# Transforming back along the rows by even and odd frequencies, with the halves as sum and difference and the poles' part included

## The chip, the cores and the metric

The kernel runs on one core of a Trainium2 chip. TensorE (PE) multiplies matrices into PSUM; VectorE (DVE), ScalarE (ACT) and GpSimd (POOL) work on SBUF, and all but POOL also on PSUM in this kernel. SyncE (SP) issues DMAs, and POOL issues some too. The metric is the device time of one execution in microseconds (us), the median of several; lower is better.

## The reference

The input is `x`, 16 images of 16 channels of 256 x 256, float32. Two layers run one after the other, each on a group-normed input and with a residual sum. The change is in layer 0, a Laplace-type layer:

```
alpha = jnp.fft.fft2(x, axes=(-2, -1))
...
output_residue1 = jnp.einsum('biox,oxik->bkox', alpha, S)
output_residue2 = jnp.einsum('bikpq,ikpq->bkpq', D, weights_residue)
x1 = jnp.fft.ifft2(output_residue1, s=(Ny, Nx), axes=(-2, -1)).real
...
F = jnp.einsum('kbpq,bipz->kbiqz', output_residue2, E1)
x2 = jnp.einsum('kbiqz,biqx->kizx', F, E2).real
return x1 + x2 / Nx / Ny
```

`x1` is an inverse transform over both axes; `x2` is the poles' part, a sum of exponentials `E1` along the rows' axis (y) times `E2` along x. Layer 1 (convolutions and a gate) follows and isn't changed; it needs `x + x1 + x2/N/N`, group-normed.

## The kernel before, in words

The program has four stages, one function each, and the change touches the first three.

`layer0_forward` norms the input, transforms it along y and then along x, and writes the spectrum `al` to DRAM. Beside that, a generator `tables` makes tables piece by piece; the last of them are the exponentials of the poles (lines 500 to 531): for each axis and each pair of channels `k` some twenty DVE operations, an exponential and a sine, and at L529 the product `arg`, 128 x 2 x 256, which goes to the DRAM table `ed`. On the axis "2" the factor `last`, +-1/(N*N), is multiplied in.

`layer0_mix` goes through 33 groups of four y frequencies, mixes channels, and transforms back along x in `columns` (L682 to L715): for each frequency `fy` and each half `q` of the batch, PE gives an even and an odd part, ACT copies the odd one (L701), DVE writes sum and difference into `o` (L704, L705; tag `h`, five buffers), and POOL issues the DMA to the DRAM array `hd` (L709; L715 for fy = 0 and 128). Here `hd` is `[128 fy, batch, channel, v, 256 x]`, where v is the real or imaginary part. In this stage the order on PE, ACT, DVE and POOL is that of the program text.

`layer0_back` (L779 to L868) transforms back along y. For each of 16 images it loads the residues `r2`, and then goes through four groups of four channels, 64 groups in all. For a group SP loads `h` (1 MB, from `hd`, one DMA) and `x` (1 MB). For each pair of channels one product with `e1` gives `pf`, which ACT copies to `f` (L834). For each channel PE makes `py`, 128 x 2 x 256: each half image `yh` takes three matmuls, two with the table `iy` over v (L839) and one with `f` and `e2` for the poles' part (L842). DVE adds `py` into `x` (L845) and takes its statistics (L846). After four channels the statistics are aggregated (L849), and `group_norm_scalars` (L30 to L54) makes mean and scale for the two norm groups: two matmuls with `ones` (L34, L42), small DVE operations of 128 x 2 (L36 to L39, L44, L47, L50 to L53) and a square root on ACT (L46). Then DVE and POOL each write two of the four channels, normed, into `z` (L856), and SP stores `z` to the DRAM array `zn` (L865). `h` and `x` have three buffers each, `py` three, `f` three, `z` three. In this stage no order is written out by hand: the framework orders the instructions of each engine when the program is built, and SP's DMAs stand in one queue.

`layer1` reads `zn`.

Of the kernel before, what the change touches and what calls it, by code (L numbers as in the profile page):

```python
# [10 lines left out]
F32 = mybir.dt.float32  # L11
I32 = mybir.dt.int32
AF = mybir.ActivationFunctionType
ALU = mybir.AluOpType
# [4 lines left out]
C = 16  # L19
N = 256  # L20
G = 8
P = 128
# [34 lines left out]
def load(nc, pool, src, shape, name):  # L57
    t = pool.tile(shape, F32, tag=name, name=name)
    nc.sync.dma_start(out=t, in_=src)
    return t  # L60
# [322 lines left out]
def tables(ctx, tc, d, psum, tabs):  # L383

    nc = tc.nc
    td, avd, ed = tabs
    cp = ctx.enter_context(tc.tile_pool(name="tc", bufs=1))
# [23 lines left out]
    for k in range(C):  # L411
        e = tp.tile([P, N], F32, tag="te", name="te")
# [89 lines left out]
    for i, axis in enumerate("12"):  # L502
        pr = cp.tile([P, C], F32, name=f"epr{axis}")
        pi = cp.tile([P, C], F32, name=f"epi{axis}")
        for a in range(2):
            nc.sync.dma_start(out=pr[64 * a : 64 * a + 64], in_=d[f"p{axis}r_kp"])
            nc.sync.dma_start(out=pi[64 * a : 64 * a + 64], in_=d[f"p{axis}i_kp"])
        tr = cp.tile([P, N], F32, name=f"etr{axis}")
        nc.sync.dma_start(out=tr, in_=d["ty" if axis == "1" else "tx"].to_broadcast([P, N]))
        for k in range(0, C, 2):  # L510
            arg = tp.tile([P, 2, N], F32, tag="arg", name="arg")
            n = tp.tile([P, 2, N], F32, tag="n", name="n")
            nf, af = n.rearrange("p k x -> p (k x)"), arg.rearrange("p k x -> p (k x)")
            for j in range(2):
                nc.vector.tensor_scalar(arg[:, j], tr, pi[:, k + j : k + j + 1], None, ALU.mult)

            nc.vector.tensor_scalar(n, arg, 1.0 / TWO_PI, phase, ALU.mult, ALU.add)
            nc.vector.tensor_scalar(n, n, ROUND, ROUND, ALU.add, ALU.subtract)
            nc.vector.scalar_tensor_tensor(af, nf, -c1, af, ALU.mult, ALU.add)
            nc.vector.scalar_tensor_tensor(af, nf, -c2, af, ALU.mult, ALU.add)  # L520
            nc.vector.tensor_scalar(arg, arg, turn, None, ALU.add)
            nc.vector.tensor_scalar(arg, arg, 3.1415925, -3.1415925, ALU.min, ALU.max)
            nc.scalar.activation(n, arg, AF.Sin)
            for j in range(2):
                nc.vector.tensor_scalar(arg[:, j], tr, pr[:, k + j : k + j + 1], None, ALU.mult)
            exponential(nc, tp, af)
            if axis == "2":
                nc.vector.tensor_scalar(n, n, last, None, ALU.mult)
            nc.vector.tensor_tensor(arg, arg, n, ALU.mult)  # L529
            nc.sync.dma_start(out=ed[:, i, k : k + 2], in_=arg)  # L530
            yield

# [15 lines left out]
def layer0_mix(ctx, tc, d, al, hd, tabs):  # L548
# [133 lines left out]
    def columns(g, f, yt):  # L682

        ph = [psh.tile([P, 2, N], F32, tag="ph", name="ph") for q in range(2)]
        for e in range(2):
            if e:
                yield
            for n, (c, v) in enumerate(((0, 0), (0, 1), (1, 0), (1, 1))):
                i = 2 * (2 * c + e) + v
                for q in range(2):  # L690
                    lanes = slice(64 * q, 64 * q + 64)
                    nc.tensor.matmul(  # L692
                        ph[q][:, e],
                        lhsT=yt[lanes, i].rearrange("p t k -> p (t k)"),
                        rhs=ix[lanes, i],
                        start=n == 0,
                        stop=n == 3,
                    )
        for q in range(2):
            odd = hp.tile([P, 2, P], F32, tag="odd", name="odd", bufs=2)  # L700
            nc.scalar.copy(odd, ph[q][:, 1].rearrange("p (v x) -> p v x", v=2))  # L701
            o = hp.tile([P, 2, 2, P], F32, tag="h", name="h", bufs=5)
            even = ph[q][:, 0].rearrange("p (v x) -> p v x", v=2)
            nc.vector.tensor_tensor(o[:, :, 0], even, odd, ALU.add)  # L704
            nc.vector.tensor_tensor(o[:, :, 1], even, odd, ALU.subtract)  # L705
            o = o.rearrange("p v h x -> p v (h x)")
            fy = 4 * g + f
            if fy % P:
                nc.gpsimd.dma_start(  # L709
                    out=hd[fy, q:nb:2].rearrange("b k v x -> b (k v x)"),  # L710
                    in_=o.rearrange("p v x -> p (v x)"),
                )
            else:
                part = fy // P
                nc.gpsimd.dma_start(out=hd[0, q:nb:2, :, part], in_=o[:, 0])  # L715

    E = mybir.EngineType
    with tc.manual_schedule(engines={E.PE, E.Activation, E.DVE, E.Pool}):
# [60 lines left out]
def layer0_back(ctx, tc, d, hd, bd, zn, mr, ed):  # L779


    nc = tc.nc
    nb = d["x"].shape[0]
    cp = ctx.enter_context(tc.tile_pool(name="bc", bufs=1))
    iy = load(nc, cp, d["iy"], [P, 2, N], "iy")
    ones = load(nc, cp, d["ones"], [P, P], "ones")

    e1 = cp.tile([P, C, N], F32, name="e1")
    e2 = cp.tile([P, C, N], F32, name="e2")
# [22 lines left out]
    for b in range(nb):  # L812
        r2 = fp.tile([P, P], F32, tag="r2", name="r2")
        nc.sync.dma_start(out=r2, in_=bd[b])
        for k0 in range(0, C, 4):
            h = hp.tile([P, 4, 2, N], F32, tag="h", name="h")
            nc.sync.dma_start(
                out=h.rearrange("p k v x -> p k (v x)"),
                in_=hd[:, b, k0 : k0 + 4].rearrange("f k v x -> f k (v x)"),
            )  # L820
            x = hp.tile([P, 4, 2, N], F32, tag="x", name="x")
            nc.sync.dma_start(
                out=x.rearrange("p k h x -> p (k h) x"),
                in_=d["x"][b, k0 : k0 + 4].rearrange("k (h p) x -> p (k h) x", p=P),
            )
            st = sm.tile([P, 4, 6], F32, tag="st", name="st")
            for k in range(4):
                if k % 2 == 0:
                    pf = psf.tile([P, 2, N], F32, tag="pf", name="pf")
                    nc.tensor.matmul(  # L830
                        pf, lhsT=r2, rhs=e1[:, k0 + k : k0 + k + 2], start=True, stop=True
                    )
                    f = fp.tile([P, 2, N], F32, tag="f", name="f")
                    nc.scalar.copy(f, pf)  # L834
                py = psy.tile([P, 2, N], F32, tag="py", name="py")
                for yh in range(2):
                    ys = slice(P * yh, P * yh + P)
                    for v in range(2):
                        nc.tensor.matmul(  # L839
                            py[:, yh], lhsT=iy[:, v, ys], rhs=h[:, k, v], start=v == 0, stop=False  # L840
                        )
                    nc.tensor.matmul(  # L842
                        py[:, yh], lhsT=f[:, k % 2, ys], rhs=e2[:, k0 + k], start=False, stop=True
                    )
                nc.vector.tensor_tensor(x[:, k], py, x[:, k], ALU.add)  # L845
                nc.vector.bn_stats(st[:, k], x[:, k].rearrange("p h x -> p (h x)"))  # L846
            mv = sm.tile([P, 2, 2], F32, tag="mv", name="mv")
            for g in range(2):
                nc.vector.bn_aggr(mv[:, g], st[:, 2 * g : 2 * g + 2].rearrange("p c s -> p (c s)"))  # L849
            g0 = k0 // 2  # L850
            nm, rs = mr[:, b, g0 : g0 + 2, 0], mr[:, b, g0 : g0 + 2, 1]
            for _ in group_norm_scalars(nc, sm, psn, ones, mv, 2, nm, rs):
                pass
            z = zbuf[(4 * b + g0 // 2) % 3]
            for g, eng in ((0, nc.vector), (1, nc.gpsimd)):
                eng.tensor_scalar(  # L856
                    z[:, 2 * g : 2 * g + 2, :, 1 : N + 1],
                    x[:, 2 * g : 2 * g + 2],
                    nm[:, g : g + 1],
                    rs[:, g : g + 1],  # L860
                    ALU.add,
                    ALU.mult,
                )
            for h in range(2):
                nc.sync.dma_start(  # L865
                    out=zn[b, k0 : k0 + 4, 1 + P * h : 1 + P * h + P].rearrange("k p x -> p k x"),
                    in_=z[:, :, h],
                )  # L868
# [433 lines left out]
def fourier_tables():  # L1302
# [33 lines left out]
    for t in tt:  # L1336
# [5 lines left out]
        "wxa": parities(wx[..., :P]),  # L1342
        "wxn": wxn,
        "ix": ix,
        "iy": iy,
        "ones": np.full((P, P), 1.0 / P),
        "pair": np.stack([np.tile(np.eye(64), (2, 1)), -np.tile(np.eye(64), (2, 1))], axis=1),
        "gc": np.tile(np.repeat(np.eye(G), 2, axis=0), (8, 1)),
# [8 lines left out]
        "m8": np.tile(np.repeat(np.eye(8), M, axis=0), (4, 1)),  # L1357
        "mt": mt.reshape(P, 2, 16),
        "phase": np.repeat([0.25, 0.0], 64)[:, None],
        "last": np.repeat([1.0, -1.0], 64)[:, None] / (N * N),  # L1360
    }
    return {name: a.astype(np.float32) for name, a in out.items()}

# [25 lines left out]
def forward(ctx, tc, d):  # L1389
# [2 lines left out]
    keep = ctx.enter_context(tc.tile_pool(name="keep", bufs=1))  # L1392
    al = dram.tile([NF, 2, 64, nb, N], F32, name="al")
    bd = dram.tile([nb, P, P], F32, name="bd")
    hd = dram.tile([P, nb, C, 2, N], F32, name="hd")
    tabs = (
        dram.tile([P, 2, C, N], F32, name="td"),
        dram.tile([NF, P, 384], F32, name="avd"),
# [34 lines left out]
```

## Time and profile before

| | us |
|---|---|
| median of 8 runs | 7631.73 |
| range of the runs | 7622.29 to 7638.18 |
| the profiled execution's time | 7629.84 |
| its span | 7628.0 |

| engine | busy us | share of the span |
|---|---|---|
| PE | 7108.3 | 93% |
| DVE | 4905.9 | 64% |
| ACT | 3670.5 | 48% |
| POOL | 2833.3 | 37% |

The profile lists, for each engine, when it was busy and what ended its idle time. It cuts the span into 40 equal slices; a digit is a busy share in tenths. Instructions of one line, engine and shape form a group, with a count, busy time, mean duration in ns, and the idle time just before them. A table by windows gives the busy time of each engine between two points of the span, the clock that PE was granted, the share of the 16 DMA engines that was busy, and what they moved.

### The profile page before, as it was taken

What the parts mean: (1) busy time and instruction counts of PE and PEld (TensorE: products, weight loads), DVE (VectorE), ACT (ScalarE), POOL (GpSimd) and SP (SyncE); (2) the same over time, 40 slices, a digit from 0 to 9 for tenths busy, and PEclk for the clock granted to TensorE, in tenths of its full rate; (3) what the DMA queues carried; (4) which work ended last, traced back from release to release, by engine and by line L of the source; (5) the groups of instructions that cost most, each with busy time, mean ns of one, the idle gap of its engine ahead of it and who ended that gap; (6) DMA issues with size and microseconds to landing.
All of it is one profiled execution on the core that took longest, in us unless ns stands there. A gap on an engine that the chain in (4) does not pass through costs nothing. (4 is left out here: it accounts for less than half of the span.)

```text
span 7628.0 us, 147451 instructions
## 1 busy us (share of the span) xinstructions
PE 7108.3 (93%) x58728; PEld 4078.4 (53%) x58728; DVE 4905.9 (64%) x9184; ACT 3670.5 (48%) x5387; POOL 2833.3 (37%) x3616
## 2 busy tenths in 40 slices
PE   7889999799999998999979999999999999999997
PEld 5778888567666666777723333333333333333332
DVE  8999865366666665666656666666666666666652
ACT  2223333366666663111156565666565666565661
POOL 2334444211111111111145555555554555554552
PEclk9999999899999999999989999999999999999998
DMA  3344444333333335877757888898888898888886
GB/s 98 111 115 122 115 120 111 108 101 96 96 95 101 100 95 163 265 242 246 230 154 220 238 241 246 246 266 256 252 245 247 245 265 256 252 246 249 244 266 199
DMA packets 936290, 1442.20 MB, mean 189 GB/s; under 512 B 91866, under 2 KB 807958, under 8 KB 903606
## 3 DMA queue, kind: packets, MB, share of 16 engines
q1 hardware_dynamic: 792374, 958.51, 45.0%
q0 software_dynamic: 143232, 474.25, 19.6%
q8 instruction: 469, 7.68, 0.4%
q14 instruction: 215, 1.76, 0.1%
HBM read 875.87 MB, written 556.47 MB: 188 GB/s over the span
## 5 line engine op out<-in xcount | busy, mean ns | idle before, releaser
L1021 ACT ACTIVATE wide<-c,b 32x512 f32<-32x512 f32 x2176 | 1477.5, 679 | 372.3 <-PE c L972 319.9
L1049 DVE TENSOR_TENSOR t<-pd,r 64x512 f32<-64x512 f32 x1088 | 744.4, 684 | 1318.7 <-PE pd L1041 1294.2
L1052 DVE TENSOR_TENSOR top<-pd,t 32x512 f32<-32x512 f32 x2176 | 1504.3, 691 | 55.6 <-DMA cf<-top 2.8
L1115 PE MATMUL c2ps<-rows,c 128*32 128x512 f32 x12288 | 1394.5, 600 | 23.4 <-ACT e L1124 13.7
L972 PE MATMUL c<-z,w 102*128 102x512 f32 x2048 | 1051.7, 645 | 138.9 <-ACT wide L1021 115.2
L1033 POOL COPY wide<-wide 32x1031 f32<-32x1031 f32 (+1 forms) x576 | 569.0, 988 | 1385.2 <-ACT wide L1021 1357.9
L1041 PE MATMUL pd<-wide,dw 128*128 128x512 f32 x2048 | 1011.9, 616 | 7.7 <-POOL wide L1034 2.7
L1115 PEld LDWEIGHTS c2ps<-rows,c 128*32 128x32 f32 x12288 | 388.6, 109 | 996.8 <-issue 892.2
L972 PEld LDWEIGHTS c<-z,w 102*128 102x128 f32 x2048 | 398.6, 197 | 701.7 <-issue 513.5
L1041 PEld LDWEIGHTS pd<-wide,dw 128*128 128x128 f32 x2048 | 376.2, 194 | 628.7 <-issue 454.2
L709 POOL DMA_DIRECT2D hd<-h x254 | 188.6, 742 | 1271.5 <-DVE h L705 1251.7
L1124 ACT ACTIVATE e<-c2ps,b 128x512 f32<-128x512 f32 x256 | 175.9, 687 | 862.2 <-PE c2ps L1115 859.5
L1034 POOL COPY wide<-wide 32x1031 f32<-32x1031 f32 (+1 forms) x576 | 572.4, 994 | 35.8
L313 PE MATMUL px<-wxn,u 128*64 128x256 f32 x4224 | 558.8, 385 | 3.0 <-ACT o L320 2.5
L839 PE MATMUL py<-h,iy 128*128 128x256 f32 x2048 | 542.2, 383 | 5.2 <-issue 5.2
L635 PE MATMUL ps<-tt,lt 128*64 128x256 f32 x4224 | 495.4, 384 | 39.6 <-DVE lt L621 36.2
L692 PE MATMUL ph<-ix,yt 64*128 64x256 f32 x4128 | 502.8, 391 | 10.2 <-issue 9.5
L313 PEld LDWEIGHTS px<-wxn,u 128*64 128x64 f32 x4224 | 401.0, 136 | 128.4 <-ACT o L320 6.6
L692 PEld LDWEIGHTS ph<-ix,yt 64*128 64x128 f32 x4128 | 393.4, 190 | 97.2 <-issue 49.9
L839 PEld LDWEIGHTS py<-h,iy 128*128 128x128 f32 x2048 | 385.6, 191 | 108.6 <-issue 50.0
L207 PE MATMUL pu<-fy,eo 128*128 128x128 f32 x2048 | 426.6, 292 | 10.8 <-DVE u L224 6.5
L594 DVE TENSOR_SCALAR alb<-alc,m 128x1024 f32<-128x1024 f32 x330 | 418.8, 1393 | 0.0
(202 smaller groups left out, 10004.7 us busy)
## 6 DMA issues: line engine op xcount, KB each, us to landing
rows<-cf SPq DMA_DIRECT2D x128, 2176.0 KB
z<-zn SPq DMA_DIRECT2D x768, 256.0 KB
cf<-top POOLq DMA_DIRECT2D x512, 240.0 KB, 7.4
cf<-bot POOLq DMA_DIRECT2D x96, 840.0 KB, 10.8
alc<-al SPq DMA_DIRECT2D x264, 256.0 KB
zn<-zb SPq DMA_DIRECT2D x128, 516.0 KB
o<-zn SPq DMA_DIRECT2D x64, 1032.0 KB
z<-in_x SPq DMA_DIRECT2D x64, 1024.0 KB
```

The source lines that it names most:

```text
L313: nc.tensor.matmul(ps[64 * k : 64 * k + 64, :, h], lhsT=u[:, h, part, g0 + j + k].rearrange("p f c -> p (f c)"), rhs=wxn[:, h, part], star ...
L635: nc.tensor.matmul(ps[64 * h : 64 * h + 64, v], lhsT=lt[:, h, k, 1 - v : 3 - v].rearrange("p l f c -> p (l f c)"), rhs=tt[:, h, k], start= ...
L692: nc.tensor.matmul(ph[q][:, e], lhsT=yt[lanes, i].rearrange("p t k -> p (t k)"), rhs=ix[lanes, i], start=n == 0, stop=n == 3,)
L839: nc.tensor.matmul(py[:, yh], lhsT=iy[:, v, ys], rhs=h[:, k, v], start=v == 0, stop=False)
L972: nc.tensor.matmul(ps[:, q], lhsT=w, rhs=cols[:, 1 - q], start=True, stop=True)
L1021: nc.scalar.activation(self.feat[64 - 32 * q : 96 - 32 * q, f, self.groups[g], :H], ps[32 * f : 32 * f + 32, q], AF.Mish, bias=b1[0][32 * ...
L1033: nc.gpsimd.tensor_copy(flat[0:32, f, 1:m], flat[64:96, f, 0 : m - 1])
L1034: nc.gpsimd.tensor_copy(flat[96:128, f, 0 : m - 1], flat[32:64, f, 1:m])
L1041: nc.tensor.matmul(ps, lhsT=dwt if self.tail else dw, rhs=self.feat[:, f, cs, :H], start=True, stop=True,)
L1049: nc.vector.tensor_tensor(t[64:128], ps[:64], self.r[:, cs], ALU.mult)
L1052: nc.vector.tensor_tensor(self.top[32 * f : 32 * f + 32, cs, q], ps[lanes], t[lanes], ALU.add)
L1115: nc.tensor.matmul(ps[32 * j : 32 * j + 32], lhsT=c2[:, blk, dx, :], rhs=t[:, 4 * j + blk : 4 * j + blk + 4, x : x + H], start=(blk, dx) = ...
```

## The change

The inverse transform along y of a half image differs between the two halves only in the sign of the odd frequencies. So the kernel after the change makes two sums per channel, over even frequencies and over odd ones, and takes their sum as the upper half image and their difference as the lower one. One matmul covers real and imaginary part of 64 frequencies at once, since both now stand on the partitions of `h`. The poles' part is put in the same form: the table on axis "1" holds half sum and half difference of its two halves.

In `tables`, two DVE operations are added per channel pair on axis "1" (16 in all); the factor 0.5 is in `last`:

```
             nc.vector.tensor_tensor(arg, arg, n, ALU.mult)
+            if axis == "1":
+                lo, hi = arg[:, :, :P], arg[:, :, P:]
+                nc.vector.tensor_tensor(n[:, :, :P], lo, hi, ALU.add)
+                nc.vector.tensor_tensor(n[:, :, P:], lo, hi, ALU.subtract)
+                arg = n
             nc.sync.dma_start(out=ed[:, i, k : k + 2], in_=arg)
```

In `layer0_mix`, each `o` is written with one DMA per part v (one alone for fy = 0 and 128), into an array whose first index is the parity of fy:

```
-            if fy % P:
-                nc.gpsimd.dma_start(
-                    out=hd[fy, q:nb:2].rearrange("b k v x -> b (k v x)"),
-                    in_=o.rearrange("p v x -> p (v x)"),
-                )
-            else:
-                part = fy // P
-                nc.gpsimd.dma_start(out=hd[0, q:nb:2, :, part], in_=o[:, 0])
+            for v in range(2):
+                if fy % P or v == 0:
+                    part = fy // P if fy % P == 0 else v
+                    nc.gpsimd.dma_start(
+                        out=hd[fy % 2, part, fy % P // 2, q:nb:2].rearrange("b k x -> b (k x)"),
+                        in_=o[:, v],
+                    )
```

In `layer0_back`, the table `iy` is half as large, `h` comes in two DMAs, and a channel has four matmuls, a copy on ACT, two sums on DVE and one on POOL:

```
-    iy = load(nc, cp, d["iy"], [P, 2, N], "iy")
+    iy = load(nc, cp, d["iy"], [P, 2, P], "iy")
...
-            h = hp.tile([P, 4, 2, N], F32, tag="h", name="h")
-            nc.sync.dma_start(
-                out=h.rearrange("p k v x -> p k (v x)"),
-                in_=hd[:, b, k0 : k0 + 4].rearrange("f k v x -> f k (v x)"),
-            )
+            h = hp.tile([P, 2, 4, N], F32, tag="h", name="h")
+            for e in range(2):
+                nc.sync.dma_start(
+                    out=h[:, e].rearrange("p k x -> p (k x)"),
+                    in_=hd[e, :, :, b, k0 : k0 + 4].rearrange("v f k x -> (v f) (k x)"),
+                )
...
-                for yh in range(2):
-                    ys = slice(P * yh, P * yh + P)
-                    for v in range(2):
-                        nc.tensor.matmul(
-                            py[:, yh], lhsT=iy[:, v, ys], rhs=h[:, k, v], start=v == 0, stop=False
-                        )
+                for e in range(2):
                     nc.tensor.matmul(
-                        py[:, yh], lhsT=f[:, k % 2, ys], rhs=e2[:, k0 + k], start=False, stop=True
+                        py[:, e], lhsT=iy[:, e], rhs=h[:, e, k], start=True, stop=False
                     )
-                nc.vector.tensor_tensor(x[:, k], py, x[:, k], ALU.add)
+                    nc.tensor.matmul(
+                        py[:, e],
+                        lhsT=f[:, k % 2, P * e : P * e + P],
+                        rhs=e2[:, k0 + k],
+                        start=False,
+                        stop=True,
+                    )
+                odd = fp.tile([P, N], F32, tag="odd", name="odd")
+                nc.scalar.copy(odd, py[:, 1])
+                o = fp.tile([P, 2, N], F32, tag="o", name="o")
+                nc.vector.tensor_tensor(o[:, 0], py[:, 0], odd, ALU.add)
+                nc.vector.tensor_tensor(o[:, 1], py[:, 0], odd, ALU.subtract)
+                nc.gpsimd.tensor_tensor(x[:, k], x[:, k], o, ALU.add)
                 nc.vector.bn_stats(st[:, k], x[:, k].rearrange("p h x -> p (h x)"))
```

`odd` and `o` have three buffers each, as `f` has. The DRAM array `hd` becomes `[2, 2, 64, batch, channel, 256]`, of the same size, and the host's table `iy` is rearranged to match.

More of the change, by code (lines that the diff above doesn't have):

```diff
@@ L1344, in fourier_tables @@
         "ix": ix,
-        "iy": iy,
+        "iy": iy[..., :P].reshape(64, 2, 2, P).transpose(2, 0, 1, 3).reshape(P, 2, P),
         "ones": np.full((P, P), 1.0 / P),
@@ L1359, in fourier_tables @@
         "phase": np.repeat([0.25, 0.0], 64)[:, None],
-        "last": np.repeat([1.0, -1.0], 64)[:, None] / (N * N),
+        "last": np.repeat([0.5, -0.5], 64)[:, None] / (N * N),
     }
@@ L1394, in forward @@
     bd = dram.tile([nb, P, P], F32, name="bd")
-    hd = dram.tile([P, nb, C, 2, N], F32, name="hd")
+    hd = dram.tile([2, 2, 64, nb, C, N], F32, name="hd")
     tabs = (
```

## The prediction

> **What bounds the kernel now.** I read the page's slices first, to see which engine is full where; then a table by windows of the stage that the change rewrites (`layer0_back`); then the order of instructions over two of its groups, for what one matmul costs; then groups by shape and waits, for prices. The slices:
>
> ```profile
> PE   7889999799999998999979999999999999999997
> DVE  8999865366666665666656666666666666666652
> PEclk9999999899999999999989999999999999999998
> DMA  3344444333333335877757888898888898888886
> ```
>
> PE is full nearly everywhere. `layer0_back` is slices 16 to 20, where the DMA row jumps from 3 to 8. By windows, for the 64 groups of four channels (columns: window, length, busy of PE, PEld, DVE, ACT, POOL, clock, DMA share, GB/s):
>
> ```profile
> 2993.00:3821.00 828.00, 825.30 (x3570) 649.08 (x3570) 510.11 (x1331) 85.95 (x188) 110.16 (x63) 1.00 0.79 246
> ```
>
> PE is busy 825 of 828 us at full clock: PE bounds this stage, at 828/64 = 12.93 us a group. But the 16 DMA engines are already at 0.79 and DVE at 510/828 = 62%. The timeline gives the matmul's price:
>
> ```profile
> 3311.24 1.03 PE L839 MATMUL py<-h,iy 128*128 128x256 f32 x4
> ...
> 3312.10 0.59 PE L842 MATMUL py<-e,f 128*128 128x256 f32 x2
> ...
> 3312.53 1.03 PE L839 MATMUL py<-h,iy 128*128 128x256 f32 x4
> ```
>
> Each f32 matmul is two instructions, and one half image (two L839, one L842) takes 3312.53 - 3311.24 = 1.29 us: 0.43 us a matmul. (The 383 ns of the group view is latency, not spacing.)
>
> **The back stage, by engine, per group.**
>
> PE. A channel falls from six matmuls to four: 8 x 0.43 = 3.45 us go. What stays: 16 x 0.43 = 6.9, two `pf` at 0.86 = 1.7, the norm's matmuls 0.9 (what is left of 12.93). PE's floor is 9.5 us.
>
> DMA. `x`, `h`, `zn` and a quarter of `r2` are 3.17 MB a group, unchanged. At today's share the engines need 0.79 x 12.93 = 10.2 us. The stage also shows them full for a while, when three early `o<-zn` loads fall in:
>
> ```profile
> 3112.00:3132.00 20.00, 19.97 (x88) 15.77 (x87) 12.81 (x31) 1.96 (x4) 3.51 (x2) 1.00 1.05 330
> ```
>
> 3.17 MB at 330 GB/s is 9.6 us; at the 299 GB/s of 3100 to 3150 it is 10.6. The trace's DMA records give an 8192-byte packet 318 ns and a 4096-byte one 160, so halving `h`'s rows to 4 KB changes nothing. DMA's floor is 9.6 to 10.6: above PE's. That alone forbids the full gain.
>
> DVE. It is busy 510/64 = 8.0 us a group. Four L845 of 692 ns go (2.8); eight sums of 256 come. The mix has that very operation:
>
> ```profile
> L704 DVE TENSOR_TENSOR h<-ph,odd 128x256 f32<-128x256 f32 x258 | 110.5, 428 | 320.9 <-ACT odd L701 320.9
> L224 DVE TENSOR_TENSOR u<-pu,right 128x256 f32<-128x256 f32 x512 | 264.9, 591 | 53.4 <-ACT right L222 53.1
> L51 DVE TENSOR_TENSOR gnt<-gnt,gnv 128x2 f32<-128x2 f32 x64 | 24.5, 383 | 0.6
> ```
>
> 428 ns, with starts 0.33 to 0.37 us apart in a row, so 8 cost 2.6 to 3.4; I take 3.0. DVE's work is then 8.2 us. To it come the norm chain's round trips to PE and ACT, before L36, L44 and L47: today 80.7 us of idle in 64 groups, 1.26 a group. The framework already puts a ready L845 between L51 and L52, so I count half, 0.65.
>
> The third row shows something else: L51 takes 383 ns in the forward stage, but 161 in the back stage. The forward timeline says why:
>
> ```profile
> 884.88 2.65 POOL L194 TENSOR_TENSOR eo<-z 128x1024 f32<-128x1024 f32 x1 [5.59 <-PE pv L214]
> ```
>
> ```profile
> 885.22 2.33 DVE L53 TENSOR_TENSOR rs<-gnr,gnt 128x2 f32<-128x2 f32 x1
> ```
>
> A 0.15 us DVE operation with two inputs in SBUF stands until POOL's tensor operation ends (887.5 both). The change puts four such operations on POOL per group. The nearest POOL row:
>
> ```profile
> L131 POOL TENSOR_TENSOR p<-pr 128x512 f32<-128x512 f32 x4 | 4.4, 1096 | 48.1 <-DVE gnr L47 17.3 <-DVE st L174 16.2 <-DMA pr<-in_p2r 13.4
> ```
>
> It lies between 726 ns at 256 elements (L265) and 2428 at 1024 (L194); I take 1.1 us. POOL then works 4 x 1.1 + 1.75 (L856) = 6.2 us a group, no bound. But its sums cover 4.4/10.7 = 41% of the time, with 0.55 us left on average, so 0.23 us for each of six exposed DVE operations (L38, L39, L50, L51, L53, L856): 1.4 us. The same rule on the forward stage (POOL's sums 17% of the time, at most 1.2 us left) gives at most 1.0 us a group for five; L38 and L50 to L53 there are 0.65 above the back stage. So 0.6 to 1.4; I keep 1.4, because the sums here are spread over the whole group.
>
> Last, `bn_stats` (L846) now waits for POOL's sum instead of DVE's own. Queued behind it on DVE are the next channel's sums, and they free `py`, of which PE has three. A following pair (0.75 us) placed ahead of it covers most of 1.1; I count 0.1 a channel, 0.4. DVE: 8.2 + 0.65 + 1.4 + 0.4 = **10.7 us**, bounds 9.5 (0.6 of port waits, POOL's sum covered) to 11.7 (428 ns a sum, no round trip filled). DVE is what ends last, just above DMA.
>
> The Trainium skill, SBUF — State Buffer, Who interferes with whom, speaks against this change: a Vector instruction with two SBUF inputs, or in a two-port mode, and a GpSimd one that reads SBUF lock each other out for the whole instruction. The pair of rows at 885 us agrees; by engine totals alone, without that rule, DVE's sum would be 9.3 and DMA would bound.
>
> GPSIMD Engine Reference, Engine selection, advises against two-input arithmetic on GpSimd as about twice as slow as Vector; here 1096 against 692 ns, 1.6 times. With the sum left on DVE, DVE would need 8.2 + 4 x 0.69 = 11.0 before any wait.
>
> The other new waits. ACT copies the odd half (L701: 383 ns); behind it on ACT stand the `f` copies and L46; ACT is busy 86 of 828 us, plus 256 x 0.38 = 97, so it costs nothing but latency. POOL's sum waits for the second DVE sum; behind it stands L856, behind that on SP the `zn` stores, then the `x` and `h` loads. These loads are issued some two groups ahead (about 21 us for 1 MB), so a delay of 2 us is hidden; without that cover it would be 2 us a group.
>
> **The rest.**
>
> The mix: `hd` goes out in 512 DMAs instead of 258. 254 x 742 ns = 188 us more on POOL, which waits 1230 us there for L705, about 17 us between pairs. Landing is 5.7 us, five `h` buffers: nobody waits; without that cover, up to 188 us. The last row (fy = 128) stays one DMA per tile, so the hand-over to the back stage keeps its time; 64 more SP issues of 0.33 us go into SP's waits.
>
> Forward: 16 sums on DVE, 0.43 (L704) to 0.69 us (L529), 7 to 11 us, where DVE is 90% busy (800 to 1000) but 54 to 67% in the next 200: bounds 0 and 11, I take 2. A gain is excluded, since work is only added. The last group's chain grows by the copy, the second sum and POOL's sum: 2. The smaller `iy` load (half) is hidden among the loads at 2973.
>
> **Sum.** Against the profiled execution's 7629.84 us (span 7628.0): -64 x (12.93 - 10.7) = -143, +2 +2: 7491. That execution lies 1.9 below the median of the eight, 7631.73: **7493 us**.
>
> **Rivals.**
>
> Forecast, DVE bounds, 9.9 to 11.7 us a group (below that DMA decides): 7442 to 7557. Chance 0.45.
>
> DMA bounds. For it: share 0.79 and a floor of 9.6 to 10.6. Against: DVE's sum is above it. At 10.2, with 10 us more for the three `o<-zn` (3.2 MB) that no longer fit in idle time: 7629.8 - 175 + 14 + 1.9 = 7471; at 9.6 to 10.6, 7433 to 7497. Chance 0.22.
>
> PE still bounds, at 9.5: 7629.8 - 220 + 6 = 7416. It needs DMA below any full window seen. Chance 0.08.
>
> DVE waits for POOL, partly uncovered: if the next pair covers only 0.7 of the 1.1, 0.4 a channel, 1.6 a group: 10.7 + 1.6 = 12.3, 7595. Chance 0.15.
>
> Slower: the order on DVE leaves each `bn_stats` directly behind its own sums, so every channel pays POOL's 1.1 us and two hand-overs of 0.1; the 0.4 counted above becomes 4 x 1.3 = 5.2, and the port waits mostly vanish: 14.5 a group, 7629.8 + 100 + 6 = 7736. It decides once more than (12.93 - 10.7)/4 = 0.56 us a channel is added to my sum. Against it: today's interleaving. Chance 0.06.
>
> No change: the gain is eaten between these two, near 12.9. Chance 0.04.
>
> **Numbers.** A measurement here tells about 0.2% (15 us) from no change. Faster 0.45 + 0.22 + 0.08 + 0.15 = 0.90, same 0.04, slower 0.06. The range 7430 to 7600 leaves out PE's floor, no change and slower, 0.18.
>
> **What would show it.** Right: in the back stage PE falls to near 90% busy, waiting for `py` buffers; DVE rises above 80%; L51 and L53 show 0.5 to 1 us beside POOL sums; POOL's sum near 1.1 us; DMA share 0.9 to 1.0. DMA bound: share 1.0, SP issues stretched to several us, PE waiting for `h`. Wrong altogether: a POOL sum near 2 us, or `bn_stats` idle of over 0.5 us a channel.

## The result and the profile after

The kernel after takes 7653.54 us, the median of 12 runs (7635.41 to 7659.3), against 7628.98 us for the kernel before beside it: a ratio of 1.0029, 95% interval 1.0021 to 1.0036. It is slower by 0.3%, where 7493 had been forecast. The profiled execution took 7655.37 us, with a span of 7653.6. In its slices, `layer0_back` is again 16 to 20:

```profile
PE   7889999789999998888869999999999999999997
DVE  8999975366666665656556666666666666666662
PEclk9999999899999999988879999999999999999998
DMA  3444444333333335777767888889888898888896
```

PE has come off its 9s there, its clock too, and the rows of DVE and DMA have hardly moved: none of them is full. The window of that stage (columns as before):

```profile
2990.00:3842.00 852.00, 692.54 (x2546) 505.80 (x2546) 517.28 (x1581) 174.41 (x443) 422.67 (x315) 0.90 0.77 236
```

The stage now takes 852 us, 13.31 a group of four channels, against 828 before. Those 24 us are the loss (the spans differ by 25.6). PE lost 1024 instructions and 133 us of busy time, and stands still for 160 us. DVE is busy 517/64 = 8.1 us a group, where its work was forecast at 8.2. So DVE's work is as forecast, and the time lies in waits. DVE's waits from 2980 to 3900 (columns: us in total, times, longest):

```profile
DVE st L862 <- POOL x L861: 167.2, 222, 1.6
DVE o L859 <- ACT odd L857: 76.0, 83, 20.2
DVE gnq L36 <- PE gn_mean L34: 39.4, 60, 3.5
DVE gnv L44 <- PE gn_var L42: 37.2, 46, 1.6
DVE gnr L47 <- ACT gnr L46: 18.2, 61, 0.5
```

They sum to 338.0 us. The longest, 20.2, is the wait for the stage's first copy, before the groups run. Without it 317.8 are left, 4.97 a group, beside 8.08 of work. Each of them ended on the result of another engine, none on a DMA. The timeline shows how one group ends on DVE, PE and POOL:

```profile
3301.88 0.69 DVE L862 BATCH_NORM_STATS2 st<-x 128x6 f32<-128x512 f32 x1 [1.26 <-POOL x L861]
...
3302.87 0.59 PE L34 MATMUL gn_mean<-mv,ones 128*128 128x2 f32 x2 [1.18 <-DVE mv L865]
3303.32 2.05 PE L839 MATMUL pf<-e,r 128*128 128x512 f32 x2
...
3305.17 0.42 PE L42 MATMUL gn_var<-gnq,ones 128*128 128x2 f32 x2
3305.45 3.76 PE L839 MATMUL pf<-e,r 128*128 128x512 f32 x4
...
3305.63 0.16 DVE L44 TENSOR_SCALAR gnv<-gn_var 128x2 f32<-128x2 f32 x1 [1.59 <-PE gn_var L42]
...
3307.18 0.81 DVE L872 TENSOR_SCALAR zb<-x,mr 128x1024 f32<-128x1024 f32 x1
3307.31 1.75 POOL L872 TENSOR_SCALAR zb<-x,mr 128x1024 f32<-128x1024 f32 x1 [5.47 <-DVE mr L53]
...
3309.01 0.85 PE L846 MATMUL py<-h,iy 128*128 128x256 f32 x2
...
3310.73 0.42 DVE L859 TENSOR_TENSOR o<-py,odd 128x256 f32<-128x256 f32 x1 [2.74 <-ACT odd L857]
3311.07 0.41 DVE L860 TENSOR_TENSOR o<-py,odd 128x256 f32<-128x256 f32 x1
...
3311.57 2.50 POOL L861 TENSOR_TENSOR x<-x,o 128x512 f32<-128x512 f32 x2 [2.51 <-DVE o L860]
```

From 3302.6, where the last statistics end, to 3310.7 DVE makes no sum; it does 2.6 us of small work, the normed write among it. I call such a group **closed**: the scalar chain (L34 to L53) and the normed write stand in DVE's queue with nothing of the next group among them. Meanwhile POOL waits 5.5 us for the chain. PE has waited 1.2 us for the aggregated statistics, and then makes `pf` for the pairs to come at half its speed (four instructions take 3.76 us), so that the next `py` begins only at 3309.0 and DVE waits once more.

The order of DVE's queue, one letter for an entry of the timeline, which runs equal neighbours together now and then (s a sum, x the sum into `x`, b statistics, a aggregation, c one chain operation, Z the normed write; three groups of each kernel):

```
before  xbaxbxbaccccccccxcbcZ xbaxbxbaccccccccxcbcZ xbaxbxbaccccccccxcbcZ
after   sssssbsssbabaccccccccccZ ssssssbbssabaccccccccccZ ssssbbssasbsbaccccccccscscsZ
```

Before, a sum and statistics of the next group stood in the chain; after, 37 of the 64 groups are closed.

### The profile page after: what moved, and what is told of

Its sections match the earlier page's. It is cut to its first block, busy times and chain, and to the rows that moved or that the text cites. A ratio compares the mean times of both kernels' runs of the same rounds, so it can differ in the third digit from the quotient of the medians.

```text
span 7653.6 us, 146762 instructions
## 1 busy us (share of the span) xinstructions
PE 6975.8 (91%) x57704; PEld 3936.4 (51%) x57704; DVE 4923.5 (64%) x9456; ACT 3758.7 (49%) x5643; POOL 3283.9 (43%) x4126
## 5 line engine op out<-in xcount | busy, mean ns | idle before, releaser
L718 POOL DMA_DIRECT2D hd<-h x512 | 323.6, 639 | 1233.6 <-DVE h L711 1209.0
L320 ACT ACTIVATE o<-px,rsc 128x512 f32<-128x512 f32 (+1 forms) x272 | 186.0, 686 | 473.7 <-PE px L313 441.1
L1006 ACT ACTIVATE bot<-c,b 128x1024 f32<-128x1024 f32 x272 | 302.9, 1114 | 223.8 <-PE c L988 213.7
```

## Experiments

The theories. **T1**: POOL's queue holds the normed write ahead of the next group's sums. **T2**: DVE's statistics wait for POOL's sum, with DVE's next sums behind them, so the two engines work in turns. **T3**: PE's clock falls to half after gaps, and that is a cause of its own. **T5**: PE's queue holds the norm's matmuls ahead of the next channels'. **T6**: too few buffers. **T8**, formed after odd_first: the chain, during which DVE makes no sums; it was narrowed later to closed groups.

The runs. "A group" is the mean distance between the starts of `gn_mean` of successive groups in the profiled execution (13.39 us for the kernel after); share is that of the DMA engines from 3100 to 3600 (0.77).

| run | us | ratio to before, 95% | a group | share |
|---|---|---|---|---|
| zb_on_vector | 7606.08 | 0.9963 (0.9949 to 0.9977) | 12.52 | 0.82 |
| sum_on_vector | 7468.88 | 0.9786 (0.9771 to 0.9800) | 10.53 | 1.01 |
| stats_without_residual | 7544.04 | 0.9883 (0.9869 to 0.9898) | 11.64 | 0.90 |
| normed_write_late | 7651.66 | 1.0025 (1.0016 to 1.0035) | 13.3 | 0.76 |
| pe_order | 7619.23 | 0.9984 (0.9975 to 0.9993) | 12.83 | 0.84 |
| dve_order | 7508.48 | 0.9842 (0.9827 to 0.9856) | 11.08 | 1.01 |
| all_order | 7669.85 | 1.0056 (1.0041 to 1.0071) | 13.62 | 0.79 |
| sum_on_vector_half_h | 7436.65 | 0.9750 (0.9734 to 0.9767) | 9.94 | 0.92 |
| odd_first | 7606.17 | 0.9967 (0.9954 to 0.9980) | 12.70 | 0.78 |
| pe_filled | 7765.96 | 1.0172 (1.0155 to 1.0189) | 15.13 | 0.69 |
| deep_buffers | 7644.44 | 1.0015 (1.0006 to 1.0025) | 13.34 | 0.78 |
| dve_order_poles_ahead | 7495.14 | 0.9822 (0.9807 to 0.9837) | 10.67 | 1.03 |
| dve_chain_in_one_piece | 7500.95 | 0.9830 (0.9815 to 0.9844) | 10.84 | 1.02 |
| dve_chain_spread | 7493.61 | 0.9818 (0.9802 to 0.9835) | 10.86 | 1.01 |
| odd_first_chain_spread | 7509.12 | 0.9839 (0.9824 to 0.9854) | 11.06 | 0.96 |
| sum_on_vector_poles_ahead | 7459.61 | 0.9774 (0.9760 to 0.9789) | 10.23 | 1.03 |
| dve_closed_late | 7581.98 | 0.9937 (0.9920 to 0.9954) | 12.12 | 0.84 |
| dve_closed_next | 7578.44 | 0.9932 (0.9917 to 0.9947) | 12.15 | 0.85 |

### One instruction moved to another engine, or hung on another input

zb_on_vector: DVE writes all four normed channels.

```
-            for g, eng in ((0, nc.vector), (1, nc.gpsimd)):
+            for g, eng in ((0, nc.vector), (1, nc.vector)):
```

> Both halves of the normed write (L872) go to DVE; POOL keeps only the four sums of a group. The changed kernel takes 13.39 us a group and 7653.5 us. Theory 1 (POOL's queue: the normed write of a group stands ahead of the next group's sums, so the whole norm chain lies in every period): the loop is broken, although DVE gets 0.8 us more; 10.5 to 11.8 us a group, 7470 to 7550 us. Theory 2 (ping-pong: on DVE each channel's statistics wait for POOL's sum, with the next channel's sums behind them): unchanged waits and 0.8 us more on DVE, 13.2 to 14 us a group, 7640 to 7700 us. Theory 3 (PE's clock, halved after idle gaps, is the loss by itself): follows the gaps, so as theory 1 or 2.

sum_on_vector: the residual sum goes from POOL to DVE.

```
-                nc.gpsimd.tensor_tensor(x[:, k], x[:, k], o, ALU.add)
+                nc.vector.tensor_tensor(x[:, k], x[:, k], o, ALU.add)
```

> The residual's sum moves from POOL to DVE, 4 x 0.69 us a group; POOL keeps its half of the normed write. Theories 1 and 2 both take POOL out of the loop: DVE is busy 8.1 + 2.8 = 10.9 us a group and ends last with its round trips, 11.2 to 12.3 us, 7515 to 7590 us. If neither holds and the transfers or the clock set the pace: no gain, 7640 us or more.

stats_without_residual: the statistics are taken of `o`, so they leave the residual out and wait for nobody.

```
-                nc.vector.bn_stats(st[:, k], x[:, k].rearrange("p h x -> p (h x)"))
+                nc.vector.bn_stats(st[:, k], o.rearrange("p h x -> p (h x)"))
```

> The statistics are taken of the transform alone (o), not of the sum with the input: this leaves the residual out of mean and variance, and takes away DVE's wait for POOL's sum. Theory 2: DVE no longer waits for POOL, about 10.7 us a group, 7470 to 7520 us. Theory 1: POOL's sums of the next group still stand behind the normed write, which still waits for the norm chain; only one sum and one hand-over leave the chain, 12 to 13 us a group, 7565 to 7630 us.

normed_write_late: POOL's order is written out, each normed write two sums later.

```
+    with tc.manual_schedule(engines={mybir.EngineType.Pool}):
...
+                    if k == 1 and last:
+                        last()
...
+                last = normed
```

> Same work. The normed write of a group is issued after the second sum of the next group, and POOL keeps the order of the text; the other engines are ordered by the framework as before. Theory 1: the norm chain leaves POOL's period, 10.3 to 11.5 us a group, 7455 to 7535 us. Theory 2: the waits of the statistics for POOL's sums stay, 13 to 13.5 us a group, 7630 to 7660 us.

T1 fell as the cause: normed_write_late changed nothing, and zb_on_vector, with the whole write on DVE, gave 47 us, outside both theories' ranges. stats_without_residual gave 110 us, between the ranges of T1 and T2: much of the loss goes with DVE's wait for POOL, though 44 of its 64 groups are closed. sum_on_vector gave 185 us, more than forecast, by adding work to the engine that had been called the bound. In its window DVE is at 448/500 and the DMA engines are full:

```profile
3100.00:3600.00 500.00, 457.40 (x1887) 343.11 (x1886) 448.45 (x1367) 124.36 (x330) 80.35 (x48) 0.97 1.01 300
```

That spoke for T2, but not alone: with the sum on DVE the framework also ordered DVE's queue anew (`xasbsasxcccbcscxcscbcscscxZ`, open).

### Orders written out by hand

pe_order writes out PE's order (the norm's matmuls behind the next group's second and third channel, the poles' product a pair ahead). dve_order writes out DVE's and changes no instruction: a channel's statistics stand behind the next channel's sums or later, the aggregation and the chain's first four operations behind the next group's second channel, the rest of the chain behind its third and the normed write behind its fourth. all_order does both, and ACT and POOL too, and gives `x` a fourth buffer. The engines that are not written out are ordered by the framework anew in every run, so their queues came out different too.

```
+    with tc.manual_schedule(engines={E.DVE}):
...
+                stats(max(2 - 1, 0))
...
+                late.append(one)
...
+                if k >= 1:
+                    next(pending, None)
...
+            pending = norm(b, k0, x, st)
```

> Same work as the changed kernel. Only PE keeps the order of the text: the norm's matmuls of a group stand behind the second and third channel of the next group, and pf one channel early; DVE, ACT and POOL are ordered by the framework. Theory 1 (normed write in front of POOL's sums) fell with normed_write_late. Theory 5 (PE's queue: gn_mean stands in front of the next channels' matmuls and waits there for statistics that come late, because POOL's sum takes longer than the framework's plan has it): 10.5 to 11.8 us a group, 7470 to 7555 us. Theory 2 (ping-pong of DVE's statistics and POOL's sums): at least 13 us, 7625 to 7660 us.

> Same work. Only DVE keeps the order of the text: the statistics of a channel stand behind the sums of the next two channels, and the norm chain behind the second and third channel of the next group; PE, ACT and POOL are ordered by the framework. Theory 2: the waits of L862 for POOL vanish, 10.5 to 11.8 us a group, 7470 to 7555 us. Theory 5 alone: gn_mean on PE waits as before or longer, 12.8 to 13.5 us, 7615 to 7660 us.

> Same work. PE, ACT, DVE and POOL all keep the order of the text: statistics two channels late, the norm chain spread over the next group's second to fourth channel, pf one channel early, x with four buffers instead of three. Theories 2 and 5 both say that the waits go: the transfers bind, 10.0 to 10.7 us a group, 7440 to 7485 us. If POOL's sums lock DVE out (the port), 11 to 12 us, 7505 to 7565 us.

dve_order won 145 us over the kernel after with the same instructions on the same engines: **order is the cause**, though not shown to be DVE's alone, since other queues moved with it. pe_order gave 34 us, where T5 had about 100 or more. Its DVE queue is open (`bssacbsscccsbscaccbcscscZ`), and a group still takes 12.83 us. all_order shows that an order can be wrong as well: there PE waits 36 times, 96.6 us in 500, for the statistics, ahead of matmuls that were ready, and its clock falls to 0.87. dve_order still had five groups of 22 us. There PE waits for a table of the poles, issued too late:

```profile
3115.54 0.56 SPq L862 DMA_DIRECT2D r<-bd  x1
...
3121.02 3.76 PE L864 MATMUL pf<-e,r 128*128 128x512 f32 x4 [6.60 <-DMA r<-bd]
```

### What is left when the order is right

sum_on_vector_half_h: sum_on_vector with half of `h` loaded and used for both parities; it leaves the odd frequencies out.

```
-            for e in range(2):
+            for e in range(1):
...
-                        py[:, e], lhsT=iy[:, e], rhs=h[:, e, k], start=True, stop=False
+                        py[:, e], lhsT=iy[:, e], rhs=h[:, 0, k], start=True, stop=False
```

> As sum_on_vector (7469 us, 10.53 us a group, DMA share 1.01, DVE 90% busy), but only the even half of h is loaded and used for both halves: this leaves the odd frequencies out, 0.5 MB of 3.17 a group. If the transfers bind sum_on_vector: the group falls to DVE's or PE's pace, 9.5 to 10.0 us, 7400 to 7440 us. If DVE binds: 10.3 to 10.6 us, 7455 to 7475 us.

dve_order_poles_ahead and sum_on_vector_poles_ahead: the 16 tables `r2` are loaded before the loop.

```
+    for b in range(nb):
+        r2[b] = cp.tile([P, P], F32, name=f"r2_{b}")
+        nc.sync.dma_start(out=r2[b], in_=bd[b])
```

> The kernel dve_order (VectorE's statistics two channels late) with the 16 images' tables of the poles (r2, 64 KB each) loaded before the stage, instead of one at a time. It tells whether the five groups of 22 us in dve_order, where PE waited 6.6 us for such a load, are that load's. If so: five times 12 us go, 7508 less 40 to 60 us, about 7450 to 7470 us and 10.1 to 10.4 us a group, at the bound of the DMA queues (share about 1.0). If the long groups come from the DMA queues being full anyway: no change, 7495 to 7515.

> sum_on_vector (7469, 10.53 us a group, DMA share 1.01) with the poles' tables loaded ahead of the stage. If the loads' lateness costs there (PE's wait for them was 20 us in 500): 10.1 us a group, 7440 to 7455 us. If the DMA queues bind: no change, 7460 to 7480 us. T2 and T8 say nothing on it.

The 22 us groups are gone, for 13 us in place of the 40 to 60 expected: the other groups grew longer, since the DMA engines are full. With half of `h` left out of sum_on_vector a group is 9.94 us, DVE 483/500 and the share 0.92. So with the sum on DVE the DMA engines bind, and DVE close behind. sum_on_vector_poles_ahead is the best kernel that leaves nothing out, 2.3% below before:

```profile
3100.00:3600.00 500.00, 468.60 (x1964) 350.32 (x1963) 466.60 (x1426) 128.46 (x343) 80.50 (x49) 1.00 1.03 313
```

### Rivals, and T2 without its round trip

pe_filled: one more matmul a channel into a spare PSUM bank.

```
+                nc.tensor.matmul(pw, lhsT=ones, rhs=e1[:, 0:2], start=True, stop=True)
```

> The kernel after with one more matmul of 128x512 a channel into a spare PSUM bank that nobody reads (0.43 us at full clock; 1.7 us a group more work on PE), nothing else changed. It tells whether the half-clocked stretches of PE are a cause of their own. T3 as a cause: with fewer gaps the clock in the window of 3100 to 3600 goes from 0.89 to 0.97 or above, and the time falls below 7640 in spite of the added work. T2 (the clock follows the gaps that the round trip makes): the clock may rise, but the group stays at 13 us or more, 7645 to 7690.

deep_buffers: `psy` 5 instead of 3, `bf` 8 instead of 3, `bs` 4 instead of 2.

```
-    fp = ctx.enter_context(tc.tile_pool(name="bf", bufs=3))
+    fp = ctx.enter_context(tc.tile_pool(name="bf", bufs=8))
```

> The kernel after with more buffers in the stage back: five PSUM tiles for py instead of three, eight of each odd, o and f instead of three, four of the small tiles instead of two; no instruction changed (the framework may put them in another order). Rival T6: PE and ACT run too few channels ahead of VectorE, so that what looks like a wait for POOL is a want of buffers: then about 11 us a group, 7500 us, with VectorE's wait for POOL below 0.2 us a channel. T2: the order of VectorE's queue is what counts and buffers do not change what stands behind the waiting statistics: 12.8 to 13.5 us a group, 7620 to 7660.

odd_first: POOL starts from ACT's copy, and DVE's statistics follow DVE's own sum.

```
+                nc.gpsimd.tensor_tensor(x[:, k, 0], x[:, k, 0], odd, ALU.add)
+                nc.gpsimd.tensor_tensor(x[:, k, 1], x[:, k, 1], odd, ALU.subtract)
+                for e in range(2):
+                    nc.vector.tensor_tensor(x[:, k, e], py[:, 0], x[:, k, e], ALU.add)
```

> The same work as the kernel after, with the round trip taken out: POOL now adds and subtracts the odd half on x itself (two instructions of half the size, which hang on ACT's copy alone), then VectorE adds the even half from PSUM (two of 128x256, as before) and takes its statistics behind its own instruction. VectorE no longer hands anything to POOL and waits for it. T2 (the round trip VectorE, POOL, VectorE in two queues served in order sets the pace): about 10.5 to 11.3 us a group and 7470 to 7520 us. T3 (it is the PE clock, with the gaps from elsewhere): no change, 7640 to 7665. A rival to T2: POOL's two instructions of half the size cost well over 0.64 us each and POOL becomes the bound; then POOL's busy share is above 80% and the group is 4 x 2 x their duration.

pe_filled added twice what was planned: such a matmul takes 0.86 us, as `pf` does, and not 0.43.

```profile
3199.70 1.02 PE L858 MATMUL pw<-e,ones 128*128 128x512 f32 x2
3200.56 1.02 PE L841 MATMUL pf<-e,r 128*128 128x512 f32 x2
```

That is 3.44 us a group. The clock rose to 0.95, and the time rose by 112 us, 1.74 a group, where T3 had it fall. But the run doesn't weigh the clock cleanly: besides the added work the framework built other queues, in which DVE's normed write takes 1790 ns instead of 874. pe_order says more: there the clock is 0.95 as well, with no work added, and a group takes 12.83 us. So the clock alone is not the loss, and its share is not shown. T6 fell: 9 us. And **T2 fell in its size**: without the round trip 47 us went, not 130 to 180. The trace of odd_first shows what was left, in the window 3100 to 3600:

```profile
POOL zb L872 <- DVE mr L53: 185.0, 39, 5.5
DVE x L861 <- POOL x L858: 102.9, 92, 2.2
```

POOL waits 4.7 us a group for the chain, with the next sums behind it, and DVE for those sums. DVE's queue is closed in 59 of 64 groups (`xxxbxbxabxbaccccccccccZ`). Hence T8, and three runs that take dve_order's two changes apart.

### Closed against open

dve_chain_in_one_piece: statistics late, the chain in one piece behind the next group's second channel.

```
-                if k >= 1:
-                    next(pending, None)
+                if k == 1:
+                    for _ in pending:
+                        pass
```

> dve_order_poles_ahead (7495, 10.67 us a group) with one thing put back: the chain of a group's scalars and the normed write stand in one piece in VectorE's queue, behind the second channel of the next group; the statistics stay two channels late. T2 (the statistics that wait for POOL's sum with the next sums behind them are the cause): 7490 to 7520 us, below 11.1 us a group. T8 (the chain, 3 to 5 us a group in which VectorE does no sums and PE stands still for want of free PSUM, is the cause): 12.3 us a group or more, 7590 to 7640 us.

dve_chain_spread: the chain spread, statistics one channel late.

```
-        stats(2)
+        stats(1)
...
-                stats(max(2 - 1, 0))
+                stats(0)
```

> dve_order_poles_ahead with the other thing put back: the statistics one channel late (behind the next channel's two sums, so that they wait for the rest of POOL's 1.28 us, about 0.5 us a channel), the chain still spread over the next group's channels. T8: 7490 to 7520 us, below 11.1 us a group, though the wait for POOL is there. T2: 4 x 0.5 us a group come back, 12.5 us a group or more, 7600 to 7640 us. If both together make the loss, each of the two runs gives a part, about 11.5 to 12 us.

odd_first_chain_spread: odd_first with the spread chain and the tables ahead (the two edits shown above).

> odd_first (7606, 12.7 us a group) with VectorE's order written out: statistics directly behind its own addition, the chain spread over the next group's channels, the poles' tables loaded ahead. T8: the chain's gap goes, about 10.3 to 10.9 us a group, 7470 to 7510 us, and POOL's wait ahead of the normed write falls below 2 us a group. T2 alone: odd_first had nothing left of it, so 7590 to 7610 us as before.

Each half of dve_order gave the whole gain, and odd_first with an open chain went from 7606 to 7509, though POOL still waits 2.8 us a group ahead of its normed write, where less than 2 was expected. So neither theory stands as forecast: the chain in one piece missed T8's 7590 to 7640, and statistics one channel late missed T2's 7600 to 7640. But all of these stand at a DMA share of 0.96 or more, which can hide a cost. What they have in common is that two channels of the next group pass ahead of the chain. The last pair closes the group and differs in the place of the statistics alone:

```
-                if k >= 1:
-                    next(pending, None)
...
-            pending = norm(b, k0, x, st)
+            for _ in norm(b, k0, x, st):
+                pass
```

> VectorE's order written out with the group closed: sums of channels 0 to 3 with the statistics two channels late, then the rest of the statistics, the chain, the normed write, and only then the next group's first sums; the poles' tables ahead. T8 (the closed group): 4 x 1.43 work, about 1.6 wait for POOL's last two sums, chain 3.2, write 0.8, together 11.4 and more where the next sums are late; 12 us a group, 7570 us or more. T2 (the wait inside the group): 11 us a group or less, 7520 us or less.

> The same with the statistics one channel late, as in the kernel after: about 0.5 us a wait more for three channels. If VectorE's order is the whole cause, this gives the kernel after back: 12.8 to 13.6 us a group, 7620 to 7660 us. If the place of the statistics costs nothing beside the closed group, it equals dve_closed_late within 15 us. If it is below 7560, VectorE's order is not the cause and something that the framework orders elsewhere is.

The queues, one group each:

```
dve_chain_spread  ssbssbaccccssbccccccssbZ
dve_closed_next   ssssbssbssbbaccccccccccZ
dve_closed_late   ssssssbssbbaccccccccccZ
```

Closing costs 12.15 - 10.86 = 1.3 us a group, 85 us in all (7578 against 7494), and the DMA share falls to 0.85. Within a closed group the place of the statistics makes no difference (7582 and 7578). DVE's waits in dve_closed_next, 3100 to 3600, and then in dve_closed_late:

```profile
DVE st L913 <- POOL x L909: 65.4, 82, 1.3
DVE gnv L44 <- PE gn_var L42: 61.1, 40, 2.9
...
DVE o L907 <- ACT odd L905: 10.2, 26, 0.6
```

```profile
DVE gnv L44 <- PE gn_var L42: 65.5, 41, 3.5
DVE o L907 <- ACT odd L905: 48.0, 67, 1.7
DVE st L913 <- POOL x L909: 24.7, 66, 0.8
```

Statistics put later save 41 us of waiting for POOL and give 38 back as waiting for ACT's copy: in a closed group, moving the statistics only moves the wait.

The largest wait that both have in common is that for `gn_var`. The timeline of dve_closed_next shows what stands ahead of it in PE's queue:

```profile
3306.57 0.38 PE L34 MATMUL gn_mean<-mv,ones 128*128 128x2 f32 x2 [0.17 <-DVE mv L832]
...
3308.26 0.70 PE L892 MATMUL py<-h,iy 128*128 128x256 f32 x2 [1.31 <-DMA h<-hd]
3308.79 0.28 PE L42 MATMUL gn_var<-gnq,ones 128*128 128x2 f32 x2
...
3309.11 0.16 DVE L44 TENSOR_SCALAR gnv<-gn_var 128x2 f32<-128x2 f32 x1 [1.58 <-PE gn_var L42]
```

The next group's first `py` waits for its `h`, 40 times from 3100 to 3600, and the chain's second matmul stands behind it. DVE waits 61.1/40 = 1.5 us a group there, against 33.4/62 = 0.5 in the kernel before. So about 1.0 of the 1.3 us passes through this wait, and no run separates it from the closing of DVE's queue. In the kernel after, PE doesn't wait for `h` in this window.

**What stays open.** dve_closed_next was to give the kernel after back, and gave 7578. The other 75 us lie in the rest of the framework's order. 13 of them may be the poles' loads (dve_order against dve_order_poles_ahead), and pe_order's 34 shows that PE's order has a part; the runs do not separate these further. Nor is it shown that closing is what costs in the kernel after: there one normed write on DVE follows the last by 13.5 us on average where it ends a closed group, and by 13.1 where it ends an open one, and pe_order and pe_filled are slow with open queues. That the order of the queues makes the loss is shown; which part of the order is not.

## Why the prediction was wrong

**PE** was right: 8 matmuls a group went, and in the fastest run (sum_on_vector_half_h) a group takes 9.94 us, of which PE is busy 478.7/500, the floor of 9.5.

**DMA** was right: beside the floor of 9.6 to 10.6 stand groups of 10.23 to 10.86 us at shares of 1.01 to 1.03. This rival becomes the bound as soon as the queues are ordered well. (The packets' 318 and 160 ns are 309 and 164 as medians of the trace's records.)

**DVE's work** was right in sum, 8.1 us against 8.2: 413 ns a sum and 693 the statistics. The other choice, the sum left on DVE, was priced too high: not 11.0 us before any wait, but 448.45/500 of 10.53 = 9.4 (sum_on_vector).

**The step that failed** is the term for waits, "A following pair (0.75 us) placed ahead of it covers most of 1.1; I count 0.1 a channel, 0.4", and with it "The framework already puts a ready L845 between L51 and L52, so I count half, 0.65". Both took the order of DVE's queue from the kernel before. A third wait was put at nothing: of ACT's copy it says "it costs nothing but latency". Measured per group: statistics waiting for POOL 2.61 (0.4 forecast), the chain's round trips 1.48 (0.65), sums waiting for ACT's copy (76.0 - 20.2)/64 = 0.87 (none), together 3.9 more than forecast. In the kernel after the framework built another order, closed in 37 groups of 64. When the order is written out as the prediction assumed, dve_order_poles_ahead gives 10.67 us a group and 7495 us, beside the 10.7 and 7493 forecast; but DVE is then busy only 355/500, and it is the DMA share of 1.03 that binds. The mechanism named for that number was not the one that binds, so that the number is met there is luck.

**Port waits**, put at 1.4, were mis-sized the other way for this kernel. In the kernel after, by groups:

```profile
L861 POOL TENSOR_TENSOR x<-x,o 128x512 f32<-128x512 f32 x256 | 323.9, 1280 | 145.6 <-DVE o L860 123.2 <-DMA h<-hd 17.7 <-DVE mr L53 3.2
L38 DVE TENSOR_TENSOR gnq<-gnq 128x2 f32<-128x2 f32 x64 | 12.4, 194 | 0.0
L51 DVE TENSOR_TENSOR gnt<-gnt,gnv 128x2 f32<-128x2 f32 x64 | 10.3, 160 | 2.1
```

Both stood at 161 ns before. Over L38, L50, L52, L53 and the write the excess is about 0.2 us a group. In a closed group POOL stands idle during the chain; in dve_order_poles_ahead it does not, and L38 and L50 show 243 and 233 ns, again about 0.2 us a group: L38 begins there at 3300.16 and stands until POOL's sum ends at 3300.36, near its end and not at a random point of it. In pe_order it is otherwise:

```profile
L39 DVE TENSOR_TENSOR gnq<-gnq,mv 128x2 f32<-128x2 f32 x39 | 45.4, 1163 | 1.3
L50 DVE TENSOR_TENSOR gnt<-gnr 128x2 f32<-128x2 f32 x39 | 25.5, 655 | 1.3
L838 DVE TENSOR_SCALAR zb<-x,mr 128x1024 f32<-128x1024 f32 x39 | 58.7, 1505 | 1.1
```

Against 161, 160 and 812 ns in the kernel before that is 2.2 us a group. So this wait, too, goes by the order, from 0.2 to 2.2 us, and a mean over the share of time that POOL is busy gives neither. POOL's sum took 1280 ns, not 1.1 us.

The Trainium skill, GPSIMD Engine Reference, Engine selection, advises VectorE for such sums; the runs agree, 7469 us against 7654, 685 ns a sum on DVE against 1280 on POOL. But with the sum left on POOL another order gives 7495, so most of that gain needs no move.

**The rival "Slower"** was nearest in sign and place, with a chance of 0.06; in size "No change", near 12.9, was nearer. The threshold of "Slower" was 0.56 us a channel added to the sum; the three waits added 3.9 a group, 0.98 a channel, and the ports gave 0.3 back. But its mechanism, statistics directly behind their own sums, is not the order that was built, and in the two closed runs the place of the statistics costs nothing.

**The mix and the forward stage** were right. The 512 stores cost POOL 323.6 us instead of 188.6, but the back stage's first matmul came at 2990.46, before 2993.09.

## What to carry to other kernels

A sum of work per engine holds only if each queue has ready work behind every wait. When a change takes a result through a second engine and back, write down the order that will stand in each queue, above all where one unit's end chain meets the next unit's start, and price the chain in one piece. Where a profile shows no engine full and the idle time of the engine that was to bind ends on other engines' results, try another order before changing the work.

## What the runs showed of the hardware

- PE's clock falls with gaps, which makes PE's own work longer: 0.90 in the stage back, where PE stands still for 160 of 852 us, against 1.00 before, where it is busy 825 of 828; and `pf` at 3.76 us for four instructions beside 2.15 in dve_order_poles_ahead. The Trainium skill, TensorE: Matmul & The Clock Gate, Part 1, calls half clock the default state that sustained activity releases; the traces agree that gaps bring a lower clock back.
- The DMA engines were full (shares of 1.01 to 1.03) at 289 to 313 GB/s in this stage's mix.
- The wait for a port goes both ways: in dve_order_poles_ahead a POOL sum that began during DVE's normed write took 1.78 us instead of 1.27, and POOL's own normed write, when DVE's began a microsecond later, took 1197 ns instead of 1676.
